# Layer 1's short form moved into layer 0's branch, with its row added in steps and PE's order pinned

## The chip, the core and the metric

The kernel runs on one core of a Trainium2 chip. The metric is the device time of one launch in microseconds (us). Five engines work side by side, each through its own list of instructions in order: PE (TensorE, matrix products), DVE (VectorE), ACT (ScalarE), POOL (GpSimd) and SP (SyncE, which here issues transfers). They wait for each other through semaphores. The profile also names PEld, PE's loading of weights, and writes a q behind an engine's name for work of its sequencer, such as branches.

## The reference, cut to what matters

Four layers follow each other, each adding to x (2 x 1024 tokens of 256 channels):

```python
x = x + L0_ffn(L0_cond(x, cond))        # shared SwiGLU + 32 routed experts, top 1
x = x + L1_ffn(L1_cond(x, cond, mask))  # attention, then gated attention of 16 experts
x = x + L2_ffn(L2_cond(x, cond))        # two mixtures of 8 experts, top 2
x = x + L3_ffn(L3_cond(x, cond))        # a mixture, then 16 experts of limited capacity
```

In layer 1's first attention the query does not depend on the token. So its scores depend on a token only through the mask:

```python
qmod = jnp.broadcast_to(qmod[:, :, None, :], (b, h, seq, e))
scores = jnp.where(mask, scores, neg)
```

If all rows of the mask are alike, every token of a batch gets the same output. The second attention of layer 1 then sees equal tokens, and what layer 1 adds is one row of 256 numbers for each batch. The inputs have such a mask.

## The kernel before

x is held twice in on-chip memory: XT, by channel (128 partitions, 2 x 2048 tokens), and Xt, by token (16 tiles of 128 tokens). Tokens are worked on in four blocks of 512 (TB). Weights pass through a ring of 20 pieces of 512 KB; a piece is loaded again when its readers are done. Instructions are placed by a scheduler that follows data dependencies and its own estimates; `_behind` (L1214) adds an order between two instructions of one engine without a wait, and `_after` a real wait.

**Layer 0** (`_layer0`, L388) routes the tokens to experts (`_route_static`, L509), scatters their rows to memory from POOL, works the shared SwiGLU (`_shared`, L1232) for blocks 0 and 1, prepares layer 1 (`_layer1_pre`, L598: projections of the condition, and `k.differ`, which counts mask elements that differ from the first row), and then works 24 slots of 128 rows, in which every expert has 96. Experts with more rows use overflow slots: `n` is read by all engines and `with k.tc.If(n > lo)` (L491) guards them. With these inputs there are none. `_layer1_experts` (L584) then issues sixteen loads of 512 KB, layer 1's q, k, v and o weights. The shared SwiGLU for blocks 2 and 3 follows, with `Combine` (L1273) in its steps: one step is one of four slices f of 128 hidden channels; in it PE makes spg and spu, ACT the silu (ssg), DVE the product sa, and PE spo. `Combine.add` gathers a tile of the experts' outputs from POOL (yg) and adds it to Xt on DVE behind the step's product; `_back` (L1263) turns a finished tile of Xt into XT by PE (ps_bk) and ACT.

**Layer 1** is guarded in the main function by a second branch (L2163): `differ > 0` takes the general form, otherwise `_layer1_one` (L679) runs, the short form. It is one chain of small products with DVE or ACT between any two:

- s_pa (scores against all tokens), s_v_t and s_v_o (sums over tokens), s_v_h, s_pq, s_pw;
- s_psc (the masked scores), s_pm, the exponential on ACT, s_z_t and s_z_o, s_z_h, s_po, s_ph: the first attention's row h;
- s_pn and s_pl (the gate's logits), about 25 small DVE operations of gating, s_pk (h times all experts' q, k and v weights, 32 products), s_pa2, s_pqk, s_pr;
- s_pc (the row by channel) and s_pb (by token, two batches).

At its end ACT adds the row to all of XT in eight operations (L911) and DVE to all of Xt in two (L914), which read s_pb in PSUM.

**Layer 2** begins with `_cond_moe` (L1586): its shared SwiGLU on XT, eight steps to a block, with the routing in the steps of the first blocks through `Lead.hook`. Its products spg and spu are again those of `_shared` (L1245), now with XT as their input.

`_warm` (L1221) issues products whose result nobody reads: 128x512 bf16 against the identity. Before the change it is used at the end of layer 3 alone.

Of the kernel before, what the change touches and what calls it, by code (L numbers as in the profile page):

```python
# [86 lines left out]
def _consts(k):  # L87
# [24 lines left out]
    k.iota16 = cp.tile([P, CAP], BF16, name="iota16")  # L112
    nc.vector.tensor_copy(k.iota16, ii)
# [8 lines left out]
    k.one16 = cp.tile([P, P], BF16, name="one16")  # L122
    nc.vector.memset(k.one16, 1.0)
# [264 lines left out]
def _layer0(k):  # L388
# [5 lines left out]
    xbuf, ybuf = k.xbuf, k.ybuf  # L394
    with ExitStack() as ctx:
# [49 lines left out]
        rows, eid, nov = _route_static(k, rp, psum, ixf, E, C, NOV, "l0")  # L445
# [9 lines left out]
        def shared(tb, hook=None):  # L455
            po = _shared(k, pool, psum, HT, tb, *shw, hook)
            for i in range(2):
                t = tb * 4 + i * 2
                nc.vector.tensor_tensor(Xt[:, t:t + 2, :], po[i], Xt[:, t:t + 2, :], ALU.add)

        def weights(src):
            ws = [k.ring.take().rearrange("p (c f) -> p c f", f=f) for f in (F, F, D)]
            for w, n in zip(ws, ("L0_r1", "L0_r3", "L0_r2")):
                nc.sync.dma_start(w, A[n][src].rearrange("o (c p) f -> p (o c) f", p=P))
            return ws

        for tb in range(2):
            shared(tb)
        _layer1_pre(k, k.pre, psum)
        _router_biases(k, psum)  # L470
# [15 lines left out]
        split.finish()  # L486
        n = nc.values_load(nov[0:1, 0:1], min_val=0, max_val=NOV)
# [12 lines left out]
        k.l1w = _layer1_experts(k)  # L500
        k.yrows = (NS + NOV) * T
        c = Combine(k, pool, psum, rows, Xt, XT, [0, 0] + [4] * 8, 2, 4)
        for tb in range(2, NB):
            shared(tb, c.hook(tb))
        k.ring.drop(hold)
        c.finish()


def _route_static(k, pool, psum, ixf, E, C, nov, name):  # L509
# [46 lines left out]
    rows = pool.tile([P, NT], U32, name=name + "_rows", tag="s_rows")  # L556
# [7 lines left out]
    eid = pool.tile([1, nov], I32, name=name + "_eid", tag="s_eid")  # L564
    nc.vector.tensor_copy(eid, ef)
    n = pool.tile([1, 1], I32, name=name + "_nov", tag="s_nov")
    nc.vector.tensor_copy(n, end[0:1, E - 1:E])
    return rows, eid, n
# [15 lines left out]
def _layer1_experts(k):  # L584

    r = k.ring.take(12).rearrange("p (n i e c f) -> n i p e c f", n=3, i=4, c=2, f=P)
    for i in range(4):
        for j, n in enumerate("qkv"):
            k.nc.sync.dma_start(r[j, i], k.A["L1_p" + n][i * 4:(i + 1) * 4]
                                .rearrange("e (c p) f -> p e c f", p=P))  # L590
    o = []
    for i in range(4):
        o.append(k.ring.take().rearrange("p (e f) -> p e f", f=D))
        k.nc.sync.dma_start(o[i], k.A["L1_po"][i * 4:(i + 1) * 4].rearrange("e p f -> p e f"))
    return r.rearrange("n i p e c f -> p n i e c f"), o


def _layer1_pre(k, pp, psum):  # L598
# [6 lines left out]
    with ExitStack() as ctx:  # L605
# [19 lines left out]
        nc.tensor.matmul(pd, k.ones, d1, start=True, stop=True)  # L625
        k.differ = pp.tile([P, 1], I32, name="l1_differ")
        nc.vector.tensor_copy(k.differ, pd)
# [51 lines left out]
def _layer1_one(k):  # L679
# [5 lines left out]
    l1w, l1o = k.l1w  # L685
    with ExitStack() as ctx:
        pool = ctx.enter_context(tc_pool(k, "l1s", 1))
        psum = ctx.enter_context(tc_pool(k, "l1sps", 2, PSUM))
# [27 lines left out]
        def by_block(w, name):  # L716

            ps = psum.tile([P, TB], F32, name=name, tag="b")
            for c in range(2):
                for g in range(4):  # L720
                    nc.tensor.matmul(ps[quad[g], :], w[:, c, g // 2, :], XT[:, c, g * TB:(g + 1) * TB],
                                     start=c == 0, stop=c == 1, skip_group_check=True)
            return ps

        def over_tokens(a, name):

            pt = psum.tile([P, 4, P], F32, name=name + "_t", tag="b")
            for j in range(4):
                nc.tensor.transpose(pt[:, j, :], a[:, j * P:(j + 1) * P], k.ident)
            at = pool.tile([P, 4, P], F32, name=name + "_at", tag="s_at")  # L730
            nc.scalar.copy(at[:, 0:2], pt[:, 0:2])
            nc.vector.tensor_copy(at[:, 2:4], pt[:, 2:4])
            ps = psum.tile([P, D], F32, name=name + "_o", tag="b")
            for j in range(4):
                for g in range(4):
                    nc.tensor.matmul(ps[quad[g], :], at[:, j, quad[g]], Xt[:, 4 * g + j, :],
                                     start=j == 0, stop=j == 3, skip_group_check=True)
            return ps

        def halves(x, name):  # L740

            ps = psum.tile([P, 2, 2, 16], F32, name=name + "_h", tag="s")
            for c in range(2):
                nc.tensor.matmul(ps[:, c].rearrange("p b h -> p (b h)"), x[:, c * P:(c + 1) * P],
                                 s2.rearrange("p b h -> p (b h)"), start=True, stop=True)
            o = pool.tile([P, 2, 2, 16], F32, name=name + "_hs")
            nc.vector.tensor_copy(o, ps)
            return o


        pa = by_block(k.u, "s_pa")
        at = pool.tile([P, TB], F32, name="s_a")
        nc.scalar.copy(at[:, 0:256], pa[:, 0:256])
        nc.vector.tensor_copy(at[:, 256:TB], pa[:, 256:TB])
        pv = over_tokens(at, "s_v")
        vp = pool.tile([P, D], F32, name="s_vp")
        nc.vector.tensor_copy(vp, pv)
        v = halves(vp, "s_v")
        pq = psum.tile([P, 2, 2, 8], F32, name="s_pq", tag="s")
        for d in range(2):  # L760
            for c in range(2):
                nc.tensor.matmul(pq[:, d], w["q"][:, c, d * P:(d + 1) * P],
                                 v[:, c, :, 8 * d:8 * d + 8], start=c == 0, stop=c == 1)
# [3 lines left out]
        pw = psum.tile([P, 2, 2, 2, 8], F32, name="s_pw", tag="s")  # L767
        for c in range(2):
            for d in range(2):
                nc.tensor.matmul(pw[:, c, d].rearrange("p b j -> p (b j)"),  # L770
                                 k.natk[:, d, c * P:(c + 1) * P],
                                 qmd[:, d].rearrange("p b j -> p (b j)"), start=True, stop=True)
# [3 lines left out]
        psc = by_block(wk, "s_psc")  # L776
        sm = pool.tile([P, TB], F32, name="s_sm")
        mx = pool.tile([P, 1], F32, name="s_mx")
        nc.vector.tensor_tensor_reduce(sm, mb, psc, 1.0, -BIG, ALU.add, ALU.max, mx)
        pm = psum.tile([P, 1], F32, name="s_pm", tag="s")  # L780
        nc.tensor.matmul(pm, sw, mx, start=True, stop=True)
# [4 lines left out]
        pz = over_tokens(sm, "s_z")  # L786
        pr1 = psum.tile([P, 1], F32, name="s_pr1", tag="s")
        nc.tensor.matmul(pr1, sw, rs, start=True, stop=True)
# [6 lines left out]
        pov = psum.tile([P, 2, 2, 8], F32, name="s_po", tag="s")  # L795
        for d in range(2):
            for c in range(2):
                nc.tensor.matmul(pov[:, d], w["v"][:, c, d * P:(d + 1) * P],
                                 zT[:, c, :, 8 * d:8 * d + 8], start=c == 0, stop=c == 1)
# [5 lines left out]
        ph = psum.tile([P, 2, 2], F32, name="s_ph", tag="s")  # L805
        for i in range(2):
            for d in range(2):
                nc.tensor.matmul(ph[:, i, :], w["o"][:, d, i * P:(i + 1) * P], o[:, d, :],
                                 start=d == 0, stop=d == 1)
# [8 lines left out]
        pn = psum.tile([P, 2], F32, name="s_pn", tag="s")  # L818
        for c in range(2):
            nc.tensor.matmul(pn, k.ones, hq[:, c, :], start=c == 0, stop=c == 1)  # L820
        pl = psum.tile([P, 2, E], F32, name="s_pl", tag="s")
        for b in range(2):
            for c in range(2):
                nc.tensor.matmul(pl[:, b, :], hb[:, c, b, :], k.sim[:, c, :], start=c == 0, stop=c == 1)
# [39 lines left out]
        pk = psum.tile([P, 3, P], F32, name="s_pk", tag="b")  # L864
        for i in range(4):
            for c in range(2):
                for g in range(4):
                    nc.tensor.matmul(pk[quad[g]], hs[:, c, 4 * i + g, :], l1w[:, :, i, g, c, :],
                                     start=i == 0 and c == 0, stop=i == 3 and c == 1,
                                     skip_group_check=True)  # L870
# [3 lines left out]
        pa2 = psum.tile([P, 2], F32, name="s_pa2", tag="s")  # L874
        nc.tensor.matmul(pa2, pks[:, 2, :], r32[:, 0:2], start=True, stop=True)
# [3 lines left out]
        pqk = psum.tile([P, 2, P], F32, name="s_pqk", tag="s")  # L879
        nc.tensor.matmul(pqk, a4.rearrange("p g r -> p (g r)"), pks[:, 0:2], start=True, stop=True)  # L880
# [11 lines left out]
        pr = psum.tile([P, D], F32, name="s_pr", tag="b")  # L892
        for i in range(4):
            for g in range(4):
                nc.tensor.matmul(pr[quad[g], :], as_[:, 4 * i + g, :], l1o[i][:, g, :],
                                 start=i == 0, stop=i == 3, skip_group_check=True)
# [3 lines left out]
        pc = psum.tile([P, 2, 2], F32, name="s_pc", tag="s")  # L900
        for c in range(2):
            nc.tensor.matmul(pc[:, c, :], row[:, c * P:(c + 1) * P], r32[:, 0:2], start=True, stop=True)
        col = pool.tile([P, 2, 2], F32, name="s_col")
        nc.vector.tensor_copy(col, pc)
        pb = psum.tile([P, 2, D], F32, name="s_pb", tag="s")
        for b in range(2):
            nc.tensor.matmul(pb[:, b, :], ab[:, b, :], row, start=True, stop=True)
        for g in range(4):
            for c in range(2):
                x = XT[:, c, g * TB:(g + 1) * TB]  # L910
                nc.scalar.activation(x, x, AF.Identity, bias=col[:, c, g // 2:g // 2 + 1])  # L911
        for b in range(2):
# [1347 lines left out]
```

## Time and profile before

| | us |
|---|---|
| median of 3 runs (1563.42, 1567.14, 1574.32) | 1567.14 |
| the profiled execution | 1562.23 |
| its span, first to last instruction | 1560.5 |
| blocks 2 and 3 of layer 0's shared SwiGLU, first spg to last ps_bk | 276.3 to 327.4 |
| layer 1's short form, s_pa to s_pb | 332.4 to 379.1 |
| layer 2's first product | 383.8 |

The profile's timeline gives for each group of instructions its start, its duration, engine, line, operation, output and inputs, and in brackets how long the engine had idled and what ended that ("issue": nothing that the profile shows). The window tables give busy time for a stretch, then PEclk, the granted TensorE clock (1.00 is full speed), the busy share of the DMA engines and GB/s. A matmul of f32 data appears as two records for each instruction. `128*32` ahead of a shape means that 32 columns of weights are in use.

### The profile page before, as it was taken

The numbers are of one execution on the slowest core, as the hardware profiler recorded it, in microseconds if no ns is written. First come the engines' busy times: TensorE is split into PE (matmuls) and PEld (weight loads), VectorE is DVE, ScalarE is ACT, GpSimd is POOL, SyncE is SP. The second block draws the span as 40 slices with busy tenths as digits, with TensorE's granted clock in tenths as the row PEclk, the third lists the DMA queues.
The fourth block names the chain that finished last, engine by engine and source line by source line (L and its number), as shares of the span: only waits on it lengthen the run. The fifth ranks groups of instructions, "written<-read, shape, count | busy, mean of one in ns | idle before, by whom it ended". The sixth has DMA issues, their size and how long they took to land. (4 is left out here: it accounts for less than half of the span.)

```text
span 1560.5 us, 23587 instructions
## 1 busy us (share of the span) xinstructions
PE 1465.7 (94%) x8602; PEld 1019.3 (65%) x8602; DVE 477.3 (31%) x1591; ACT 303.6 (19%) x641; POOL 285.4 (18%) x317
## 2 busy tenths in 40 slices
PE   6879999976999999999999999999999999998897
PEld 2543333433555787555599999999995558864675
DVE  3732222223411354341121111111113514456432
ACT  2312221112111212111111111111111212125222
POOL 0410000300132242023101011010110073410342
PEclk9879999987999999999999999999999999998799
DMA  9759995813211286051142434354607257672470
GB/s 249 268 187 322 342 350 191 273 57 122 75 48 55 73 275 205 28 196 48 41 138 79 175 121 150 127 181 160 207 15 258 97 187 251 214 222 70 145 248 21
DMA packets 184243, 252.48 MB, mean 162 GB/s; under 512 B 17111, under 2 KB 137823, under 8 KB 184112
## 3 DMA queue, kind: packets, MB, share of 16 engines
q1 hardware_dynamic: 164448, 210.92, 41.3%
q0 software_dynamic: 14176, 36.63, 6.5%
q10 hardware_dynamic: 5488, 3.25, 0.7%
q8 instruction: 74, 1.21, 0.3%
q14 instruction: 57, 0.47, 0.1%
HBM read 284.86 MB, written 50.76 MB: 215 GB/s over the span
## 5 line engine op out<-in xcount | busy, mean ns | idle before, releaser
L1255 PE MATMUL spo<-ring,sa 128*128 128x256 f32 x768 | 191.9, 392 | 13.8 <-DVE sa L1252 13.8
L285 POOL DMA_INDIRECT tbuf<-ys,sdst x114 | 112.2, 984 | 506.7 <-ACT ys L1517 381.9
L1255 PEld LDWEIGHTS spo<-ring,sa 128*128 128x128 f32 x768 | 140.1, 191 | 95.6 <-DVE sa L1252 75.7
L1252 DVE TENSOR_TENSOR sa<-ssg,spu 128x512 f32<-128x512 f32 x96 | 65.9, 686 | 336.7 <-PE spu L1245 329.7
L1510 DVE TENSOR_TENSOR fa<-fsg,fpu 128x512 f32<-128x512 f32 x72 | 49.5, 687 | 315.9 <-PE fpu L1505 315.9
L1505 PE MATMUL fpu<-xsT,ring 128*128 128x128 f32 x1152 | 140.4, 275 | 0.0
L1505 PE MATMUL fpg<-xsT,ring 128*128 128x128 f32 x1152 | 140.3, 275 | 0.0
L1505 PEld LDWEIGHTS fpg<-xsT,ring 128*128 128x128 f32 x1152 | 137.1, 192 | 1.8
L1505 PEld LDWEIGHTS fpu<-xsT,ring 128*128 128x128 f32 x1152 | 134.4, 192 | 0.0
L1514 PE MATMUL fpo<-ring,fa 128*128 128x256 f32 x576 | 130.3, 379 | 0.0
L1250 ACT ACTIVATE ssg<-spg 128x512 f32<-128x512 f32 x96 | 57.3, 597 | 343.2 <-PE spg L1245 333.0
L1514 PEld LDWEIGHTS fpo<-ring,fa 128*128 128x128 f32 x576 | 106.7, 190 | 13.0
L1245 PE MATMUL spg<-HT,ring 128*128 128x512 f32 x192 | 99.9, 608 | 5.3 <-PEq L491 3.1
L1245 PE MATMUL spg<-XT,ring 128*128 128x512 f32 x192 | 98.4, 604 | 4.7 <-ACT XT L911 4.7
L1245 PE MATMUL spu<-HT,ring 128*128 128x512 f32 x192 | 92.0, 600 | 0.0
L1245 PE MATMUL spu<-XT,ring 128*128 128x512 f32 x192 | 91.6, 600 | 0.0
L1481 PE MATMUL cph<-xsT,ring 128*128 128x128 f32 x624 | 83.9, 278 | 4.1 <-DMA ring<-in_L_r 1.3
L1481 PEld LDWEIGHTS cph<-xsT,ring 128*128 128x128 f32 x624 | 76.0, 192 | 8.0 <-DVE ys L1490 3.2
L1488 PE MATMUL cpo<-ring,ch 128*128 128x256 f32 x312 | 80.2, 380 | 0.8 <-ACT ch L1484 0.8
L1509 ACT ACTIVATE fsg<-fpg 128x512 f32<-128x512 f32 x72 | 43.0, 597 | 169.7 <-PE fpg L1505 169.7
L1245 PEld LDWEIGHTS spu<-XT,ring 128*128 128x128 f32 x192 | 37.0, 193 | 44.4 <-issue 43.9
L1245 PEld LDWEIGHTS spu<-HT,ring 128*128 128x128 f32 x192 | 36.7, 194 | 42.7 <-issue 42.6
(570 smaller groups left out, 1644.8 us busy)
## 6 DMA issues: line engine op xcount, KB each, us to landing
ring<-in_L_w SPq DMA_DIRECT2D x108, 1024.0 KB
ring<-in_L_r SPq DMA_DIRECT2D x96, 512.0 KB
ring<-in_L_r SPq DMA_DIRECT2D x156, 256.0 KB
xs<-xbuf SPq DMA_DIRECT2D x138, 129.0 KB
ring<-in_L_W SPq DMA_DIRECT2D x32, 512.0 KB
yt<-tbuf SPq DMA_DIRECT2D x48, 256.0 KB
xbuf<-ACC SPq DMA_DIRECT2D x1, 6063.0 KB
ring<-in_L_s SPq DMA_DIRECT2D x6, 512.0 KB
```

Of the source, the lines that this page charges most:

```text
L285: i = k.nc.gpsimd.indirect_dma_start(out=self.ap, out_offset=bass.IndirectOffsetOnAxis(ap=idx, axis=0), in_=rows, in_offset=None, **end)
L1245: mm = nc.tensor.matmul(ps, W[:, c, f * P:(f + 1) * P], X[:, c, cols], start=c == 0, stop=c == 1)
L1250: nc.scalar.activation(sg, pg, AF.Silu)
L1252: mul = nc.vector.tensor_mul(a, sg, pu)
L1255: mm = nc.tensor.matmul(po[g // 2][:, g % 2, :], a[:, g * P:(g + 1) * P], W2[:, f, :], start=f == 0 and g % 2 == 0, stop=f == nf - 1, skip ...
L1481: made = [nc.tensor.matmul(ph[:, f, :], R1[:, c, f * P:(f + 1) * P], xT[:, c, :], start=c == 0, stop=c == 1) for f in range(2) for c in ra ...
L1488: made = [nc.tensor.matmul(po, h[:, f, :], R2[:, f, :], start=f == 0, stop=f == 1) for f in range(2)]
L1505: made = [nc.tensor.matmul(ps[:, j, :], W[:, c, (f0 + j) * P:(f0 + j + 1) * P], xT[:, c, :], start=c == 0, stop=c == 1) for ps, W in ((pg, ...
L1509: nc.scalar.activation(sg, pg, AF.Silu)
L1510: nc.vector.tensor_mul(a[:, f0:f0 + 4, :], sg, pu)
L1514: made = [nc.tensor.matmul(po, a[:, f, :], W2[:, f, :], start=f == 0, stop=f == 4 * nh - 1) for f in range(4 * nh)]
```

## The change

- `_layer0` adds the two counts (differing mask elements and overflow slots) to one number and branches once on it, behind the 24 slots. The arm taken with these inputs holds blocks 2 and 3 of the shared SwiGLU with `Combine`, and then the short form, with no branch between them. The other arm holds the overflow slots, a copy of the two blocks, and the old second branch with the general form and a copy of the short form.
- `_layer1_one` gets the last product ahead of it and puts each of its own products behind the one before (`pe`). Between them `fill(n)` puts n products of `_warm`, 50 in all. PSUM tiles come from layer 0's pool.
- The sixteen expert loads wait for the product sa of the first step of block 2 (`_layer1_loads`).
- The row is written to HT, which is free by then (`_layer1_sums`). `_layer1_add` adds it to XT's first block ahead of layer 2, and to the rest behind the silu and the product of layer 2's first four steps (`k.late`).
- The constants iota16 and one16 are made in layer 3's `Last` instead of at the start; what the arms share (rows, eid, the counts) moves to a longer-lived pool.

```diff
+        rare = k.pre.tile([1, 1], F32, name="l0_raref")
+        nc.vector.tensor_tensor(rare, k.differf[0:1, :], end[0:1, E - 1:E], ALU.add)
...
+    def rest():
+        c = Combine(k, pool, psum, rows, Xt, XT, [0, 0] + [4] * 8, 2, 4)
         for tb in range(2, NB):
-            shared(tb, c.hook(tb))
-        k.ring.drop(hold)
-        c.finish()
+            step = c.hook(tb)
+            def hook(f, mul, mm):
+                if tb == 2 and f == 0:
+                    _layer1_loads(k, mul)
+                step(f, mul, mm)
+            shared(tb, hook)
+        return c.finish()
+
+    def one(ref):
+        _shared_loads(k, k.l2, "L2_s1", "L2_s3")
+        _layer1_one(k, psum, ref)
+        _shared_loads(k, k.l2[2:], "L2_s2")
+
+    rare = nc.values_load(any_[0:1, 0:1], min_val=0, max_val=1 << 21)
+    with k.tc.If(rare > 0) as cmp:
...
+    with cmp.Else():
+        with tc_pool(k, "l0p", 2) as pool, tc_pool(k, "l0ps", 4, PSUM) as psum:
+            one(rest())
+    _layer1_add(k)
...
+def _layer1_loads(k, ref):
...
+            d = k.nc.sync.dma_start(r[j, i], k.A["L1_p" + n][i * 4:(i + 1) * 4]
+                                    .rearrange("e (c p) f -> p e c f", p=P))
+            _after(k, d, [ref.ins.name])
...
+def _layer1_add(k):
+    nc, (col, row) = k.nc, _layer1_sums(k)
+    def by_channel(g, ref=None):
+        for c in range(2):
+            x = k.XT[:, c, g * TB:(g + 1) * TB]
+            i = nc.scalar.activation(x, x, AF.Identity, bias=col[:, c, g // 2:g // 2 + 1])
+            if ref is not None:
+                _behind(k, i, ref)
+    def by_token(g, ref):
+        x = k.Xt[:, 4 * g:4 * g + 4, :]
+        _behind(k, nc.vector.tensor_tensor(x, x, _bc(row[:, g // 2, :], 1, [P, 4, D]), ALU.add), ref)
+    by_channel(0)
+    k.late = [lambda a, m: (by_channel(1, a), by_channel(2, a), by_token(0, m)),
+              lambda a, m: (by_channel(3, a), by_token(1, m)),
+              lambda a, m: by_token(2, m), lambda a, m: by_token(3, m)]
...
+    def pe(i):
+        nonlocal last
+        if last is not None:
+            _behind(k, i, last)
+        last = i
+    def fill(n):
+        nonlocal last
+        if last is not None:
+            last = _warm(k, psum, last, n, tag="o", bufs=2)
...
+        fill(4)
         pa = by_block(k.u, "s_pa")
+        fill(2)
...
+                pe(nc.tensor.matmul(pl[:, b, :], hb[:, c, b, :], k.sim[:, c, :], start=c == 0, stop=c == 1))
+        fill(14)
...
-        for g in range(4):
-            for c in range(2):
-                x = XT[:, c, g * TB:(g + 1) * TB]
-                nc.scalar.activation(x, x, AF.Identity, bias=col[:, c, g // 2:g // 2 + 1])
-        for b in range(2):
-            x = Xt[:, b * 8:(b + 1) * 8, :]
-            nc.vector.tensor_tensor(x, x, _bc(pb[:, b, :], 1, [P, 8, D]), ALU.add)
+        fill(6)
+        nc.scalar.copy(rows, pb)
...
+    def hook(f, mul, mm):
+        if k.late:
+            k.late.pop(0)(k.silu, mul)
+        lead_.hook(f, mul, mm)
```

The fillers ahead of each product, in order: s_pa 4, s_v_t 2, s_v_o 1, s_v_h 2, s_pq 1, s_pw 1, s_psc 1, s_pm 3, s_z_t 4, s_z_o 1, s_z_h 2, s_po 1, s_ph 2, s_pn 1, s_pk 14, s_pa2 2, s_pc 2, and 6 behind s_pb.

## The prediction

> **What bounds the kernel now.** I first read the page's engine rows: TensorE (PE) is busy for 94% of the span, so only stretches where PE idles or runs at a lowered clock can give time. The clock row shows where one of them lies: the ninth and tenth slices (312 to 390 us) have 8 and 7.
>
> ```profile
> PE 1465.7 (94%) x8602; PEld 1019.3 (65%) x8602; DVE 477.3 (31%) x1591; ACT 303.6 (19%) x641; POOL 285.4 (18%) x317
> PEclk9879999987999999999999999999999999998799
> ```
>
> Then I read PE's timeline around layer 1's short form (start, duration, what ran, and in brackets the idle time before it).
>
> ```profile
> 271.32 1.94 PE L1559 MATMUL fpo<-ring,faT 128*32 128x256 f32 x32 [0.52 <-DVE faT L1552]
> 276.32 2.74 PE L1245 MATMUL spg<-HT,ring 128*128 128x512 f32 x4 [3.06 <-PEq L491]
> ...
> 332.42 3.36 PE L721 MATMUL s_pa<-XT,l_u 128*32 128x512 f32 x16 [5.03 <-issue]
> ...
> 344.74 3.64 PE L721 MATMUL s_psc<-XT,s_wk 128*32 128x512 f32 x16 [0.28 <-DVE s_wk L774]
> ...
> 366.74 6.71 PE L868 MATMUL s_pk<-ring,s_hs 128*32 128x384 f32 x64 [3.60 <-DVE s_hs L863]
> ...
> 383.82 3.75 PE L1245 MATMUL spg<-XT,ring 128*128 128x512 f32 x4 [4.74 <-ACT XT L911]
> 387.36 3.19 PE L1245 MATMUL spu<-XT,ring 128*128 128x512 f32 x4
> ```
>
> The reader is to see four losses: 3.06 us at the overflow branch, 5.03 us at the mask branch, a serial chain of small products from 332.42 to 379.08, and 4.74 us in which PE waits for layer 1's row to be added everywhere. The first two are branches; the sequencer's rows give their length:
>
> ```profile
> L491 PEldq COMPARE_BRANCH  x1: 3608/3608/3608, 272.4 to 272.4; - x1
> L2163 PEldq COMPARE_BRANCH  x1: 4992/4992/4992, 327.4 to 327.4; - x1
> ```
>
> Last I cut the stretch into windows of 3.41 us, the steps in which the granted clock changes (length, PE busy, clock, DMA share, GB/s).
>
> ```profile
> 338.79:342.20 3.41, 2.55 (x32) 1.00 0.02 5
> 342.20:345.61 3.41, 2.86 (x16) 0.50 0.00 0
> 345.61:349.03 3.42, 2.77 (x16) 0.50 0.00 0
> 349.03:352.44 3.41, 1.56 (x16) 1.00 0.00 0
> 352.44:355.85 3.41, 2.91 (x32) 0.50 0.01 2
> ```
>
> The clock is whole or half, and half for much of the short form and for layer 2's first products, though PE counts as busy for most of each window. What differs before a drop is how many columns stream: the window from 338.79 holds 32 records, mostly of 16 to 32 columns.
>
> **The change part by part.** Durations are from the profiled execution (1562.23 us, span 1560.5).
>
> *Branches.* PE's 5.03 us before s_pa go. In their place stand four fillers and the last copy of XT, which ended at 327.80; s_pa can start about 0.9 us after the last ps_bk (327.39): -4.1. The remaining branch jumps further: past the overflow slots, the general form and a copy of the short form. L491 skipped only the overflow slots in 3.61 us, L2163 the general form in 4.99. I take the long jump's row, +1.4 (bounds 0 and +2). DVE stood 5.74 us after its long jump; then it now does eleven set-up operations, 3.1 us by their rows (332.26 to 335.4). Its next work, sa, comes 5.5 us after PE's first product, so DVE is ready some 2 us in time. Net -2.7. A rule speaks against any gain: the Trainium skill's "Advanced Engine Details and Errata" (Control Flow Timing) prices a compare-and-branch at about 108 ns. By it this part would be worth 0.1 us; PE's rows of 3.6 and 5.0 us decide.
>
> *Pinned order and fillers.* The built order shows the short form's products in the same sequence as before, so the pin moves none; it fixes where the 50 fillers stand (each 128x512 bf16). The trace has such fillers at L1225, ten in 4.45 us at half clock, 0.43 each from start to start; bf16 products of that width stand 0.21 us apart at full clock (1440.85, 1441.06). They stand in gaps of 0.27 to 3.60 us. At full clock almost all fit (two in 0.61, four in 1.28, fourteen, 3.0 us, in 3.60); at half clock they overrun the gaps by some 5.4 us, 2.4 of it by the fourteen. If they held the full clock throughout, s_pa and s_psc would take 1.92 as fpg does (16 records) at full clock: -1.4 and -1.7; s_z_o would take s_v_o's 1.94 instead of 3.31: -1.4; s_pw and s_pl would take s_pq's 1.06 instead of 1.9: -0.8 each; s_pk 5.76 (64 records of 0.09) instead of 6.71: -0.95; s_pm and s_pn about -0.4. Sum -7.4. A rule of the skill again speaks against it: "TensorE: Matmul & The Clock Gate" (Part 1) has the half rate follow an idle window of about 3.4 us. No gap inside the short form but s_pk's 3.60 is that long, so by the rule the chain would be at full clock already and the fillers would buy perhaps 1 us. The windows above decide otherwise: half clock after gaps of 0.3 us. But they also tell what it takes to stay whole. Counting 0.43 us for a 128x512 f32 record at full clock (four in 1.88) and a quarter of it for 32 columns of weights, the window from 376.33 streamed 1.1 us and kept the clock, that from 338.79 0.9 and lost it. From s_v_o to s_psc about 4.2 us hold five fillers (1.1 us); from s_z_o to the fourteen about 6 us hold six (1.3 us). So I expect two or three windows at half clock still. Stepping the chain through such windows from all phases gives a mean gain of 3.5 net of overruns; bounds -7.4 and +2.
>
> *The row added in steps.* The PSUM rows s_pb were held until DVE's two 2.28 us adds ended at 383.6, and ACT did eight adds in 5.01 us. Now ACT copies the rows out (about 0.6, by ssg's 0.60 for 128x512), then makes two adds (0.63 each); the first product needs only the first at its start. With 0.2 us twice for passing on, PE starts about 1.85 us after s_pb instead of 4.74: -2.9 (bound -0.9 if leaving the branch costs PE its 3.35 us of L1754; PE's sequencer stood at the next block's L1245 already at 377.5, so I take none). The other six ACT adds (3.8 us) go behind layer 2's first two silus, and four DVE adds of 1.14 us behind its first four muls. Steps there take 5.2 us, in which ACT works 0.60 and DVE 0.69, so they are hidden; without that cover they would cost 3.8. Queued behind them is layer 2's routing on DVE, late by up to 2 us, with three blocks (over 100 us) of cover. The logits wait for the last ACT add, done a step before PE reaches them.
>
> *Layer 2's first products* ran at half clock, 3.75 and 3.19. At full clock the same rows take 1.88 each: -3.2. Idle before them is now below 2 us, half of it filled; I take -3.0 (bounds -3.2, 0).
>
> *Weights behind the first step.* Sixteen 512 KB DMAs leave SP about 6 us later than at 276.20. At the 347 GB/s of that stretch they need 24 us, ending near 308 instead of 300, and s_pk needs them at about 355. Behind them on SP stand layer 2's first weights, which anyway waited until 321.3 for ring space. POOL's sixteen gathers, at the head of its queue, get the DMA engines alone for their first four. Groups two and three now lie wholly under the loads. Such gathers landed in up to 5.9 us, and the mul behind group two came 0.75 late (PE idle 0.69 at 305.79). One such delay more: +0.5 (bounds 0, +2).
>
> *Elsewhere.* In the routing the built order lets DVE do l_done and others in the 1.7 us for which sa waited at 52.26, so l_rows comes about 0.7 earlier, and with it scatters, slots and all behind them: -0.5 (bounds -0.7, +0.5). Two small DVE operations for the new flag, and two constants made later: nothing, DVE is busy 31%.
>
> Sum: -2.7 - 3.5 - 2.9 - 3.0 + 0.5 - 0.5 = -12.1 us; the profiled execution would go from 1562.2 to 1550.1. The runs shown (1563.42, 1567.14, 1574.32) lie above it; the middle of all four times is 1565.3, so I predict 1553.
>
> **The rivals.** *The fillers do not hold the clock:* nothing from the short form (+1 for overruns) and nothing from layer 2's first products: -2.7 + 1.0 - 2.9 = -4.6, 1560.7. For it: ten fillers in a row at 1455.8 ran at half clock to their end. Against it: there the windows before held products of 32 columns alone. *The clock holds throughout:* -2.7 - 7.4 - 2.9 - 3.2 - 0.7 = -16.9, 1548.4. For it: the windows from 335.37 to 342.20 stayed whole with 2.3 to 2.6 us busy. Against it: the two thin stretches named above. *Slower, by the gathers under the weights:* DVE's adds for one step stand ahead of the next sa, so every microsecond by which a group lands later stops PE for one, in three steps. To eat 12.1 us each group must land 4 us later, near 10 us. The longest landing that the trace has for this kind of gather is 8.3, the median 4.7; DMA share is already 1.1 in that stretch in both forms. Taken at 11 us it gives 3 x 5.1 - 12.1 = +3.2, 1568.5.
>
> **How the numbers follow.** Forecast 52% (its own range 1549 to 1558), clock not held 20%, held throughout 22%, slower 6%. Runs differ by some 1%, which is about what a measurement can tell from no change. Faster by over 1% means below 1551.5: most of the 22% and two fifths of the forecast, 0.42; slower by over 1%: 0.06, with what I have not seen; within 1%: 0.52. The range, 1546 to 1562, takes in both clock cases.
>
> **What would show it.** PE's branch row near 5.0 us at the one remaining branch and no idle over 1.5 us before s_pa; 3.4 us windows at half clock inside the short form down from seven to two or three; s_psc and s_z_o below 2 us; under 2 us of idle before layer 2's first spg, and that group at 1.9; gathers landing under 7 us. I am wrong if s_pk starts late because fourteen fillers ran at half clock, if layer 2's first products are still at half clock, or if sa waits on yg by more than 1 us a step.

## The result, and the profile after

| | before | after |
|---|---|---|
| median of 7 runs each, side by side (us) | 1570.61 (1563.42 to 1574.32) | 1555.13 (1553.40 to 1558.53) |
| the profiled execution | 1562.23 | 1554.72 |
| its span | 1560.5 | 1553.0 |

The ratio is 0.9907 (95% interval 0.9889 to 0.9926): 15.5 us, 0.9% faster, with the bound of 1% inside the interval. The time lies where it was predicted (1553, range 1546 to 1562), but the prediction took 12.1 us from a base of 1565.3, and the runs took 15.5 from one of 1570.6. The two profiled executions differ by only 7.5. So three numbers for one effect have to be brought together.

I read the engine rows and the clock row first.

```profile
PE 1470.2 (95%) x8649; PEld 1021.0 (66%) x8652; DVE 478.2 (31%) x1596; ACT 303.9 (20%) x642; POOL 285.2 (18%) x317
PEclk9989999999999999999999999999999999999799
```

The dip to 8 and 7 in the ninth and tenth slices is gone. Then PE's timeline, around the branch and through the short form:

```profile
272.66 3.27 PE L1360 MATMUL spg<-HT,ring 128*128 128x512 f32 x4 [2.77 <-issue]
...
302.53 2.00 PE L1370 MATMUL spo<-ring,sa 128*128 128x256 f32 x8 [1.35 <-DVE Xt L395]
...
310.10 1.99 PE L1370 MATMUL spo<-ring,sa 128*128 128x256 f32 x8 [1.26 <-DVE sa L1367]
...
326.20 1.92 PE L824 MATMUL s_pa<-XT,l_u 128*32 128x512 f32 x16
...
336.15 1.93 PE L824 MATMUL s_psc<-XT,s_wk 128*32 128x512 f32 x16
...
349.41 1.87 PE L941 MATMUL s_pl<-l_sim,s_hb 128*128 128x16 f32 x8
351.11 5.12 PE L1340 MATMUL warm<-ident 128*128 128x512 bf16 x14
356.17 5.37 PE L986 MATMUL s_pk<-ring,s_hs 128*32 128x384 f32 x64
...
368.55 1.96 PE L1360 MATMUL spg<-XT,ring 128*128 128x512 f32 x4
370.34 1.88 PE L1360 MATMUL spu<-XT,ring 128*128 128x512 f32 x4
```

The wait of 5.03 us ahead of s_pa and that of 4.74 ahead of layer 2 are gone, s_psc and layer 2's first products run at full clock, and longer waits stand at 302 and 310 us. The windows show the two half windows that are left, from 348.25 to 355.08 (length, PE busy, clock, DMA share, GB/s):

```profile
341.43:344.84 3.41, 3.13 (x39) 1.00 0.00 0
344.84:348.25 3.41, 3.09 (x22) 1.00 0.00 0
348.25:351.67 3.42, 3.21 (x15) 0.50 0.02 5
351.67:355.08 3.41, 3.41 (x10) 0.50 0.00 0
355.08:358.49 3.41, 3.41 (x38) 1.00 0.00 0
```

So the changed stretch gained much more than 7.5 us. Matching PE's products one by one, the changed kernel is 3.8 us ahead at 90 us (times of the kernel before), 17.0 at layer 2's first spu, 16.7 at 1166 us and 14.6 at 1250 us, then only 3.2 at 1340 us, and 7.5 at the end. Most of the loss lies in layer 3's first blocks, which the diff does not touch:

```profile
1248.43 2.90 PE L1370 MATMUL spo<-ring,sa 128*128 128x256 f32 x8 [3.58 <-issue]
...
1275.16 2.00 PE L1370 MATMUL spo<-ring,sa 128*128 128x256 f32 x8 [2.71 <-DVE sa L1367]
```

### The profile page after: what moved, and what is told of

It is laid out like the page before. It is cut to its first block, busy times and chain, and to the rows that moved or that the text cites. A ratio compares the mean times of both kernels' runs of the same rounds, so it can differ in the third digit from the quotient of the medians.

```text
span 1553.0 us, 23694 instructions
## 1 busy us (share of the span) xinstructions
PE 1470.2 (95%) x8649; PEld 1021.0 (66%) x8652; DVE 478.2 (31%) x1596; ACT 303.9 (20%) x642; POOL 285.2 (18%) x317
## 5 line engine op out<-in xcount | busy, mean ns | idle before, releaser
L1599 PEld LDWEIGHTS cph<-xsT,ring 128*128 128x128 f32 x624 | 76.0, 192 | 10.4 <-DVE sn L1527 4.8
```

What stands on the lines that cost most here:

```text
L1599: made = [nc.tensor.matmul(ph[:, f, :], R1[:, c, f * P:(f + 1) * P], xT[:, c, :], start=c == 0, stop=c == 1) for f in range(2) for c in ra ...
```

## The experiments

They are in three sets; kernels of one set ran beside each other, with the kernel before among them. My theory was the prediction's: each part gives its own term. The rivals were that the fillers do nothing, that waits only move, and that the change costs time in layer 3.

### Set 1: the kernel before again, and three parts undone

*e1, the kernel before, unchanged.*

> The kernel before, unchanged, run and profiled once more. The profile of the changed kernel gave back some 8 us between 1240 and 1340 us (layer 3's lead blocks) that the medians do not show: they differ by 15.5 us, the two profiled spans by 7.5. Theory A (the first profile of before was a lucky one; layer 3's first blocks vary from run to run in either kernel): this profile has a longer span, 1566 to 1572, and its extra time sits in 1240 to 1340 us, with PE idle there. Theory B (the change itself slows layer 3): this profile's stretch from 1240 to 1340 is within 2 us of the first profile's, and extra time, if there is any, sits elsewhere. Ratio to the kernel before 1.00 within 0.3%. It also tells whether the 3 us won before 90 us come from the change or from the run: under chance, sa's wait near 85 us differs between the two profiles of before by over 2 us.

Measured: ratio 1.001 (0.9993 to 1.0027), single times from 1556.00 to 1573.38, span 1562.2. The profile had no long wait between 1240 and 1340 us either. That is theory B's sign and not theory A's, but e2, e3 and e4 hold the changed code and lacked those waits too, so layer 3 stayed undecided until the later sets. The early part spoke against chance: sa's wait at 92 us was 6.52 us as in the first profile (6.46).

*e2, no fillers.*

```diff
     def fill(n):
-        nonlocal last
-        if last is not None:
-            last = _warm(k, psum, last, n, tag="o", bufs=2)
+        return
```

> The changed kernel with its order pinned but no fillers in layer 1's short form. Theory A (the fillers hold the clock): windows at half clock inside the short form go from two back to six or seven; from s_pa's start to s_pb's end 45 to 47 us instead of 40.95; layer 2's first spg and spu take 6.5 to 7 us instead of 3.84; in all 7 to 9 us slower than the changed kernel, 1562 to 1564 where that has 1555. Rival (the pinned order alone, or the full rate ahead of s_pa, keeps the clock; the fillers do nothing): that stretch stays within 1 us of 41, layer 2's first two groups at 3.9, in all within 1.5 us of the changed kernel, or faster by the 1.2 us by which the fourteen fillers made s_pk late.

Measured: ratio to before 0.9947 (0.9931 to 0.9964), against 0.9907 for the change. Its timeline:

```profile
338.30 3.46 PE L823 MATMUL s_psc<-XT,s_wk 128*32 128x512 f32 x16 [0.28 <-DVE s_wk L885]
...
345.40 3.58 PE L841 MATMUL s_z_o<-Xt,s_z_at 128*32 128x256 f32 x32 [0.40 <-ACT s_z_at L836]
...
360.95 7.77 PE L985 MATMUL s_pk<-ring,s_hs 128*32 128x384 f32 x64 [3.60 <-DVE s_hs L980]
...
375.64 3.37 PE L1359 MATMUL spg<-XT,ring 128*128 128x512 f32 x4 [1.29 <-ACT XT L754]
```

From s_pa to s_pb it took 46.41 us, as long as before (46.66), though the order was still pinned; layer 2's first two groups took 5.40 instead of 3.67. The fillers alone hold the clock, and the pin alone gives nothing. From the last ps_bk to the end of layer 2's first two groups e2 took 53.1 us and the change 46.8, so the fillers, overruns and all, were worth 6.3 us (5.0 and 5.2 against its later profiles e6 and e10).

*e3, the weights not made to wait.*

```diff
-            _after(k, d, [ref.ins.name])
...
-        _after(k, d, [ref.ins.name])
```

> The changed kernel with layer 1's sixteen weight loads not made to wait for the trailing block's first step: SP issues them right at the branch, as before. Theory A (gathers under the weights land late, sa waits for yg): the idle times of 1.35, 1.26 and 0.85 us ahead of PE's products at 302, 310 and 321 us fall by 1.5 to 2.5 us together, s_pa starts at 324.0 to 324.7 instead of 326.2, in all 1.5 to 2 us faster, 1553. Rival (the gathers are late by themselves, through POOL's pace or the rows they fetch, whatever the loads do): the waits only move to other steps of the two blocks, s_pa within 0.5 us of 326.2, no change in all. Prediction's own size: 0.5 us.

Measured: ratio 0.9907 (0.9877 to 0.9938), the same as with the wait. The waits at 302 and 310 us went, as theory A said (0.85 at the end of block 3 stayed). But PE's jump at the branch grew by 2.7 us, and took it all back. First PE, then its sequencer's row, of e3:

```profile
277.81 3.75 PE L1358 MATMUL spg<-HT,ring 128*128 128x512 f32 x4 [5.61 <-issue]
```

```profile
L533 PEldq COMPARE_BRANCH  x1: 6168/6168/6168, 271.5 to 271.5; - x1
```

And the same row of the changed kernel:

```profile
L533 PEldq COMPARE_BRANCH  x1: 3468/3468/3468, 269.0 to 269.0; - x1
```

The same jump at the same place costs 3.47 us when layer 1's weights wait, and 6.17 with their loads under way. Neither theory had that. It turned my reading of the branches over, and e5 was made for it.

*e4, the row added at once.*

```diff
-        nc.scalar.copy(rows, pb)
+        for g in range(4):
+            for c in range(2):
+                x = XT[:, c, g * TB:(g + 1) * TB]
+                nc.scalar.activation(x, x, AF.Identity, bias=col[:, c, g // 2:g // 2 + 1])
+        for b in range(2):
+            x = Xt[:, b * 8:(b + 1) * 8, :]
+            nc.vector.tensor_tensor(x, x, _bc(pb[:, b, :], 1, [P, 8, D]), ALU.add)
...
-    k.late = [...]
+    k.late = []
```

> The changed kernel with layer 1's row added as before: eight adds on ACT and two on DVE out of the PSUM tile, all ahead of layer 2. Theory A (the PSUM rows held until DVE's two 2.28 us adds kept PE waiting): idle ahead of layer 2's first spg, its fillers not counted, goes from about 1.4 back to 4 to 5 us after s_pb, that is +2.9 us as in the prediction's sum, and the first two groups fall to half clock for a part of their time, +1 to +3 more; in all 3 to 6 us slower, 1558 to 1561. Rival (PE would have waited anyway, for its sequencer at the branch's end or for ACT's first add): less than 1 us slower.

Measured: ratio 0.9926 (0.9899 to 0.9953), and in the trace:

```profile
374.86 3.65 PE L1363 MATMUL spg<-XT,ring 128*128 128x512 f32 x4 [3.44 <-ACT XT L1029]
```

From s_pb's end to spg 4.73 us instead of 1.40 (+3.33), and the first two groups 5.37 instead of 3.67 (+1.70), since PE's idle time costs the clock as well. 5.0 us in the trace; theory A held there. The medians alone could not tell it from the change (0.9926 beside 0.9907).

### Set 2: the branch, the change again, two repairs

*e5, the kernel before with layer 2's first weights kept until the short form has begun.*

```diff
-            _shared_loads(k, k.l2, "L2_s1", "L2_s3")
             _layer1_one(k)
+            _shared_loads(k, k.l2, "L2_s1", "L2_s3", behind=k.first)
```

> The kernel before, with one thing changed: layer 2's first two weight loads wait for the short form's first copy (about 336 us) instead of going out at 321.26 us, 6 us ahead of PE's jump at L2163. In the changed kernel PE's jump, though longer, took 3.3 to 3.5 us in three profiles, and 6.17 us in the one where sixteen loads went out right at the branch. Theory A (PE's time at a branch is set by the loads in flight while it jumps, not by how far it jumps): the jump at L2163 falls from 4.99 and 5.07 us to 3.3 to 3.6, s_pa's idle time from 5.0 to 3.4 to 3.7, and the kernel gains up to 1.5 us. Rival (the distance, or what stands at the target, sets it): L2163 stays at 4.9 to 5.1 us.

Measured: ratio 0.9993 (0.9975 to 1.0011), too coarse for 1.5 us; the row decides:

```profile
L2165 PEldq COMPARE_BRANCH  x1: 3559/3559/3559, 328.9 to 328.9; - x1
```

3.56 us instead of 4.99 (5.07 in e1), and 3.60 of idle time ahead of s_pa instead of 5.03. The jump's distance is unchanged. What made it longer before were two loads that SP issued at 321.26 and that were still landing. Theory A held.

The traces also show how. The profile has two DMA queues that it calls "instruction", and at each long jump one packet of 16 KB comes on queue q8. Here are the queues in the first 2.6 us of the jump at L2163, before and then in e5 (packets, MB, share of the 16 engines):

```profile
q1 hardware_dynamic: 243, 1.00, 94.6%
q14 instruction: 1, 0.01, 0.7%
```

```profile
q8 instruction: 1, 0.02, 3.0%
q14 instruction: 2, 0.02, 2.5%
```

With the loads landing, the q8 packet began 2.68 us into the jump (2.73 in e1), and 3.45 us into the jump of e3. In the other 24 long jumps of the twelve profiles it began after 0.93 to 1.07 us. In all 27, PE's branch row ended 1.29 to 1.57 us after that packet. So the loads lengthen the jump by holding this packet back. That it carries PE's own code is inferred from the queue's name and from this timing.

*e6, the changed kernel again, beside e5, e7 and e8.*

> The changed kernel, unchanged, as the measure for the runs beside it, and profiled once more. In the first profile of it some 8 us were lost between 1240 and 1340 us, and 3 us less than in the other profiles were lost before 90 us; three kernels with the same code in those places had neither. Theory A (both were that one run's): this profile has no idle time of PE over 1 us in layer 3's blocks there, and sa's waits before 90 us cost 3 us more; the span is 1546 to 1552. Rival (they belong to the changed kernel): both are there again. Ratio to the kernel before 0.989 to 0.993.

Measured: ratio 0.9902 (0.987 to 0.9935), medians 1559.24 and 1573.63, span 1557.1. Theory A failed here: the waits in layer 3 were there again (5.04 and 2.54 us). But e5, a form of the kernel before, had them too (4.73 and 2.02), and so had e7 and e8, while no profile of set 1 had this pair. So the rival that they belong to the change failed as well.

*e7, the second half of the weights behind block 3's second step.*

```diff
-                if tb == 2 and f == 0:
-                    _layer1_loads(k, mul)
+                if (tb, f) in ((2, 0), (3, 1)):
+                    _layer1_loads(k, mul, tb - 2)
```

> The changed kernel with layer 1's sixteen weight loads in two parts: eight behind block 2's first step as now, eight behind block 3's second step (about 309 us), so that the gathers' groups two and three, from 290 to 306 us, have the DMA engines to themselves. Theory A (weights in flight make the gathers late): PE's waits for sa at 302 and 310 us (1.35, or 1.26, in the other profiles, beside 0.85 at the blocks' ends) fall below 0.4 together, the branch stays at 3.3 to 3.5 us, 0.9 to 1.3 us faster than the changed kernel. Rival (POOL's own pace of 1.25 us a gather and four buffers of yg set it): waits within 0.3 us of the changed kernel's, no gain. Should the later half come too late, s_pk waits for its weights and the kernel is slower.

Measured: ratio 0.9895 (0.986 to 0.9929). DVE's adds show the gathers; first the changed kernel, then e7:

```profile
296.56 0.42 DVE L1403 TENSOR_TENSOR Xt<-Xt,yg 128x256 f32<-128x256 f32 x1 [1.74 <-DMA yg<-ybuf,l_rows]
297.90 0.43 DVE L1403 TENSOR_TENSOR Xt<-Xt,yg 128x256 f32<-128x256 f32 x1 [0.92 <-DMA yg<-ybuf,l_rows]
299.11 0.43 DVE L1403 TENSOR_TENSOR Xt<-Xt,yg 128x256 f32<-128x256 f32 x1 [0.78 <-DMA yg<-ybuf,l_rows]
300.26 0.43 DVE L1403 TENSOR_TENSOR Xt<-Xt,yg 128x256 f32<-128x256 f32 x1 [0.73 <-DMA yg<-ybuf,l_rows]
```

```profile
299.10 1.51 DVE L1403 TENSOR_TENSOR Xt<-Xt,yg 128x256 f32<-128x256 f32 x4 [1.00 <-DMA yg<-ybuf,l_rows]
```

Under the weights the four rows land 1.2 us apart, without them all lie ready together. PE's wait near 303 us went, but one of 1.38 us came at 312.14, where DVE began sa 1.4 us after its inputs with no transfer to wait for. Theory A's own sign, both waits together below 0.4 us, did not come, so this run alone settled nothing in time.

*e8, five more fillers.*

```diff
         v = halves(vp, "s_v")
-        fill(1)
+        fill(2)
...
         zT = halves(z, "s_z")
-        fill(1)
+        fill(2)
```

(and one more each behind s_z_o, s_po and s_ph)

> The changed kernel with five more fillers: one each behind s_v_h, s_z_o, s_z_h, s_po and s_ph, in the two thin stretches. By the windows of 3.41 us of four profiles, a window that streams 0.97 us of columns or less is followed by half clock, one with 1.08 or more is not; the thin window ahead of s_pl streams 0.84 to 0.97, and with four fillers more 1.7. Theory A (a window's streamed columns decide): no half window from s_pa to s_pb, or one; s_pl 1.06 us instead of 1.87, the fourteen fillers 3.0 to 3.1 us instead of 4.5 to 5.1, s_pk within 0.4 us of its s_hs instead of 1.2 us late; from s_pa to s_pb 38.5 to 39.5 us instead of 41; 1.5 to 2.5 us faster than the changed kernel. Rival (an idle gap or the kind of product decides, or the added fillers overrun their gaps): the half windows stay, or the stretch is 40.5 us or longer.

Measured: ratio 0.9909 (0.9875 to 0.9942). From s_pa to s_pb 40.37 us, where e6 beside it took 42.30. The half windows ahead of s_pk went, one stayed ahead of s_psc (3.23 us). Between my two numbers: the theory's direction held, and the first thin stretch needed more.

### Set 3: both repairs

*e9: e7 with the later half behind block 3's third step, and e8 with one more filler each behind s_v_o, s_pq and s_pw.*

```diff
-                if tb == 2 and f == 0:
-                    _layer1_loads(k, mul)
+                if (tb, f) in ((2, 0), (3, 2)):
+                    _layer1_loads(k, mul, tb - 2)
...
         pv = over_tokens(at, "s_v")
-        fill(2)
+        fill(3)
```

> The changed kernel with both repairs: thirteen... eight more fillers than it in the thin stretches (behind s_v_o, s_v_h, s_pq, s_pw, s_z_o, s_z_h, s_po and s_ph one each), and the second half of layer 1's weights behind block 3's third step (about 315 us), where the last gathers have landed. Theory A (a window of 3.41 us that streams about 1.0 us of columns or less costs the next its clock; weights in flight spread the gathers' landings): no half window from s_pa to s_pb, s_psc 1.93 us, that stretch 38.9 to 39.6 us where the changed kernel took 40.95 and 42.30; PE's wait near 303 us (1.35, 1.43) gone, that at the blocks' end (0.85) left; with DVE's own late start near 312 us (seen once, 1.38, with nothing missing) not there, 3.5 to 4.5 us faster than the changed kernel beside it. Rival for the fillers (a product's kind or the gaps decide): s_psc stays above 3 us. Rival for the loads (DVE or POOL's pace): a wait of 1.2 us or more at 303 or 312 us stays. The medians will hardly tell 4 us of 1557 from run to run, so the verdict rests on the trace's stretches.

*e10, the changed kernel beside it.*

> The changed kernel unchanged, as the measure beside the repaired one, and a third profile of it: s_pa to s_pb 41 to 42.5 us with two or three half windows, the wait near 303 us 1.3 to 1.5, PE's jump 3.3 to 3.6 us. Idle time of PE over 0.3 us between 1225 and 1350 us has been 4.0 to 6.3 us in five profiles and 10.4 to 12.4 in five, one of them of a form of the kernel before. If that belongs to the run and not to the change, this profile falls in either group together with the other one of this call. Ratio to the kernel before 0.989 to 0.993.

Measured: e9 1543.62 us, ratio 0.9900 (0.9878 to 0.9922); e10 1544.07, ratio 0.9902 (0.9882 to 0.9922). In the trace e9 took 39.51 us from s_pa to s_pb, e10 42.08, and e9 had no wait but the 0.85 in blocks 2 and 3. Its jump, however, took 4.53 us against 3.79. Its lead, 3.6 us at layer 2's first product, was lost at layer 3's branch, where PE stood 2.09 us between its first products and two windows ran at half clock; e10 had neither there. So each repair does what it says, but the 3.5 to 4.5 us expected of both did not come: they give nothing that the medians can show. e9's windows say why even its fillers left one half window:

```profile
341.67:345.09 3.42, 3.42 (x32) 1.00 0.00 0
345.09:348.50 3.41, 3.41 (x26) 1.00 0.02 5
348.50:351.92 3.42, 3.42 (x10) 0.50 0.00 0
```

PE counts as busy for all of the window from 345.09, and yet the next one is at half clock. Counting 0.43 us for a 128x512 f32 record at full clock, others by their columns, half for bf16 and a quarter for 32 columns of weights, it streamed 0.98 us.

In layer 3 the profiles now fell in two groups. PE's busy time in the same 125 us of the first profile of before, of the change, and of e10:

```profile
1225.00:1350.00 125.00, 120.19 (x579) 1.00 0.63 203
```

```profile
1225.00:1350.00 125.00, 113.00 (x562) 0.99 0.61 191
```

```profile
1225.00:1350.00 125.00, 120.93 (x636) 1.00 0.66 204
```

Idle time over 0.3 us in it was 3.8 to 6.2 us in seven profiles (before, e1, e2, e3, e4, e9, e10) and 10.4 to 12.4 in five (the change, e5 to e8). All of set 2 was in the second group, none of sets 1 and 3, and each group holds both kernels. It belongs to the runs and not to the change. What it is stays open: no profile names a wait for it. Each set ran on another chip, with the kernel before at 1565.42, 1573.63 and 1559.40 us, so the chip may be the cause as well as the time of the run; nothing here parts the two.

## Why the prediction was right, and where it was not

By stretches of PE, the change against the first profile of before, in the three profiles of it (the first, e6, e10):

| step of the prediction | predicted | measured |
|---|---|---|
| branches: idle at the branch, and ahead of s_pa | -2.7 | -4.5, -4.5, -4.2 |
| pinned order and fillers, s_pa to s_pb | -3.5 | -5.7, -4.4, -4.6 |
| the row added in steps, s_pb to spg | -2.9 | -3.3, -3.3, -3.3 |
| layer 2's first products | -3.0 | -3.1, -3.1, -3.1 |
| weights behind the first step, blocks 2 and 3 | +0.5 | +1.7, +0.5, +0.4 |
| sum of these | -11.6 | -15.0, -14.8, -14.9 |
| elsewhere: the routing in layer 0 | -0.5 | -1.8 |

Together -16.7 us, beside 15.5, 14.4 and 15.3 between the medians that were taken side by side. Against e1, the second profile of before, the five steps sum to -12.8 to -13.0, and with the last row to some -14.7; two of the three medians lie between these readings, the third 0.3 us below. The profiled executions' 7.5 is the odd one: the change's profile has the 7 us of waits in layer 3 that the profile of before lacks. The mechanism was right in each part but one, the price of the jump, and the sizes of the branches, the fillers and the part elsewhere were too small.

*Branches.* The term that failed is "+1.4" for the longer jump, and with it the sign "PE's branch row near 5.0 us". Measured with the weights behind block 2's first step: 3.47 us, and 3.37, 3.31, 3.52, 3.47, 3.31, 4.53 and 3.79 in e2, e4 and e6 to e10, where L491 took 3.61, 3.47 and 4.37 in the three profiles of before. The row of 4.99 was long because weights were landing, not because of what it skipped (e3, e5). The two rows of 4.4 and 4.5 us had no such loads: in them another 16 KB packet came just ahead on q8, and the last one itself took 1.7 and 2.0 us instead of 0.9 to 1.4. I had taken the right rows and put the wrong cause to them. The rule of the Trainium skill ("Advanced Engine Details and Errata", Control Flow Timing, about 108 ns) is contradicted for PE by every one of these rows.

*Pinned order and fillers.* The prediction was "two or three windows at half clock still": two, three and three. A window that starts at one moment or another of the chain decides whether s_psc runs in 1.93 or 3.64 us, which is the spread from -5.7 to -4.4. The sign said to show me wrong, "if s_pk starts late because fourteen fillers ran at half clock", came in part: they took 5.12 us, and s_pk began 1.25 us after its s_hs. Against the rule of "TensorE: Matmul & The Clock Gate" (Part 1), half the rate after an idle window, the windows decide: over twelve profiles, every window at full clock from 318 to 395 us in which I count less than 1.07 us of streamed columns was followed by half the clock, none with more than 1.30 was, and between these both were seen. PE counted as busy for 3.09 and 3.41 us in the two windows shown above that lost the clock.

*The row in steps, and layer 2's first products.* Right to 0.4 and 0.1 us. e4 brings back 3.3 of the first and 1.7 of the second. The second depends on where the window falls: in e1 those groups took 5.10 instead of 6.74, so against that profile it is -1.4.

*Weights behind the first step.* In e2, e4, e6, e8 and e10 PE's waits for sa in these blocks were 2.1 to 2.3 us together, where three profiles of before had 1.3 to 1.5: "one such delay more", of about 0.8. The first profile of the change had two (3.5 in all). The sign "if sa waits on yg by more than 1 us a step" thus came, but in one or two steps of the eight. What I did not see is what the edit buys: without it the jump costs 2.7 us more.

*Elsewhere.* "-0.5" was bounded at -0.7, and the bound was wrong. DVE's sa near 90 us stands behind l_ne, which waits for a mask load, which on SP stands behind a load that needs the last scatter. PE's row in e1, then in e10:

```profile
92.50 3.78 PE L1255 MATMUL spo<-ring,sa 128*128 128x256 f32 x8 [6.52 <-DVE sa L1252]
```

```profile
87.77 3.78 PE L1370 MATMUL spo<-ring,sa 128*128 128x256 f32 x8 [4.73 <-DVE sa L1367]
```

6.31 to 6.52 us in three profiles of before (e5 among them), 4.03 to 5.04 in nine with the changed code. The first scatter comes 10.7 to 12.2 us after l_cum's product instead of 12.2 to 12.6, on average 1.1 and not the 0.7 that I took from one wait. The rest I had not looked at: from the last scatter's start to the load that needs it, 2.6 to 3.0 us instead of 4.4 to 4.7. Why that is shorter is open. This part was not undone by itself, so its cause is argued from the rows, not shown.

*The base.* I took 1565.3, the middle of four times; seven gave 1570.6. The profiled execution, 1562.23, was faster than all seven, and it is one without the waits in layer 3. That 1553 came within 2.1 us of 1555.13 is partly luck: the base was 5.3 us too low and the effect 3.4 us too small, and the two cancel in part. In the third set the changed kernel's median, 1544.07, lay below the range.

*The rivals.* "The fillers do not hold the clock" fell with e2, "the clock holds throughout" with the half windows. "Slower by the gathers": their landings did spread under the weights, but by about 1 us and not by the 4 us a group that would have decided.

## What to carry to other kernels

Before taking a branch's price from a row, look at what the DMA engines carry while the engine jumps, and at when the instruction packet comes; weigh what bulk loads gain by going out ahead of the jump against what they add to it (here the two were about equal, e3). To keep PE's clock in a chain of small products, count streamed columns per window of 3.4 us, not busy time, and place fillers in the thinnest windows rather than in the widest gap. And take the effect of a local change from its own stretches, in two or three profiles of each kernel: here the difference between two whole profiled spans was half of the true one.

## What was not expected of the hardware

- PE's jump over the same code took 3.47 us with the weights kept back and 6.17 with them in flight, another 3.56 and 4.99; a longer distance did not lengthen it. It ended 1.3 to 1.6 us after a 16 KB packet of the instruction queue in all 27 jumps, and loads in flight held that packet back by 1.6 to 2.5 us. Without such loads it still varied from 3.3 to 4.5 us, with that packet.
- After a window in which PE was busy for 3.41 of 3.41 us the clock still fell to half; about 1 us of streamed columns in it was too little (e9).
- Layer 3's first blocks lose some 7 us in whole sets of runs and not in others, in both kernels. In them engines start late with nothing missing in the profile ("issue", 3.58 us; "remote").
